# Attention in blocks of three key tiles instead of two, with VectorE adding to two heads at once

## The chip, the cores and the metric

The kernel runs on one core of one Trainium2 chip. The metric is device time in microseconds of one execution. Before the change it is 10870.94 us, the median of 3 runs (10868.82 to 10871.01).

## The reference: what is computed

Four graph layers over N = 3327 nodes of 128 features, each `x = x + layer(relu(layernorm(x)), adj)`. The change touches only the second, an attention with 128 heads of depth 8, which sees the dense adjacency matrix as a bias, added twice:

```python
q = (x @ Wq.T).reshape(d, n, h)      # d = 128 heads, n = 3327 nodes, h = 8
k = (x @ Wk.T).reshape(d, n, h)
v = (x @ Wv.T).reshape(d, n, h)
a = jnp.einsum('dnh,dmh->dnm', q, k) * scale
a = a + adj + adj
a = jax.nn.softmax(a, axis=2)
out = jnp.einsum('dnm,dmh->dnh', a, v)
```

That is 128 x 3327 x 3327 exponentials. The other layers are products with the adjacency matrix, a gated unit and a nearest-neighbour graph; they lie ahead of and behind the attention and are not touched.

## The kernel before, in words

**Tiling.** Keys lie on the 128 partitions: 26 tiles (T) of 128 keys. Queries lie along the free dimension in 7 chunks (QW = 476; the last has 471, rounded up to 472). Heads go in 32 groups of four; a head has 32 partitions of TensorE's rows (its keys in f16 high and low parts), so four heads' score products stand in separate row groups. The loops run over chunk c, group g, tile t: 7 x 32 x 26 steps (L920, L931).

**A step.** For each head of a tile, TensorE makes a 128 x 476 block of scores (L873), twice the adjacency tile `a2` (bf16, scaled) is added, ScalarE takes the exponential, and TensorE weighs the values with it into `acc` (L904; four heads in one PSUM bank, an f32 product in two passes). A column of ones among the values gives the denominators; the division comes later.

**Pairs.** Two tiles share a buffer `p8` of 8 places (4 buffers). The adjacency reaches the scores in three ways. *Early* heads, all four of the even tile and head 3 of the odd one: the product goes into one of four PSUM banks named `early`, and VectorE adds `a2` while it copies to `p8` (L876); one exponential of five heads in place (L897). *Late* heads, 0 to 2 of the odd tile: the products go into the three banks of `late` (one buffer); for `3 - n_g` of them TensorE adds the adjacency with a product by twice the identity, `two_i` (L892); one exponential straight from PSUM (L894); for the other `n_g` POOL multiplies the result by `e`, the exponential of the adjacency tile (L896). `n_g` is 2, and 1 in the first five pairs of a group of chunk 0, where POOL has other work. `e` is made by ScalarE once per odd tile and chunk, in the last group of the chunk before (`exp_of`, L557, called in L986).

```python
if t % 2 == 0:
    early = [ps.tile([P, 512], F32, name="early", bufs=4) for _ in range(4)]
...
nc.scalar.activation(p8[:, 5:8, :we], late[:, :, :we], AF.Exp, scale=1.0 / S_SCALE)
...
nc.scalar.activation(p8[:, :5, :we], p8[:, :5, :we], AF.Exp, scale=1.0 / S_SCALE)
```

**Order.** The stage is under a manual schedule (L918): each engine works its instructions in the order in which the program writes them, and semaphores hold back only what depends on another engine. A tile is weighed six tiles after its scores (`ahead`, L948). After the last tile of a group VectorE copies `acc` to `o4` (L913), which SyncE stores; the next group's first weighing waits for that copy. All eight PSUM banks are in use: 4 early, 3 late, 1 acc.

**What else is in the queues.** In chunk 0 only: each pair's keys are brought into tile order by VectorE (`key_pair`, L653; POOL does one pair in 13), seven pairs ahead, and stored for the later chunks (L620); and POOL parts the keys and queries of a coming group into f16 high and low (`Parting`, L586 and L587): loads of both raw sides behind tile 15, the parts at tiles 2 to 9, the stores behind tile 11. In all chunks but the last, POOL doubles the next chunk's adjacency tiles (L285) and sums them (L296), SyncE loads a group's queries, values and keys some tiles ahead (L951, L975).

Of the kernel before, what the change touches and what calls it, by code (L numbers as in the profile page):

```python
# [15 lines left out]
ALU = mybir.AluOpType  # L16
# [40 lines left out]
def kernel(  # L57
# [506 lines left out]
    SIDES = ((kf, kt, "k"), (qf, qt, "q"))  # L564

    class Parting:
# [8 lines left out]
        def load(self, side):  # L575
            src, _, name = SIDES[side]
            self.raw[side] = kq0.tile([E * JW, WJ], F32, name=f"raw_{name}")
            nc.sync.dma_start(self.raw[side], self.rows(src, 0))

        def part(self, side, i):  # L580
            if i == 0:
                self.hi[side] = kq0.tile([E * JW, WJ], F16, name=f"hi{side}")
                self.lo[side] = kq0.tile([E * JW, WJ], F16, name=f"lo{side}")
# [10 lines left out]
        def at(self, t):  # L594

            for side in range(2):
                t0 = 2 + 4 * side
                if t0 <= t < t0 + 4:
                    self.part(side, t - t0)
                if t == 11:  # L600
                    self.store(side)

# [43 lines left out]
    def key_pair(engine, k_ins, pairs):  # L646
# [3 lines left out]
        k = kq0.tile([P, 2, P], F16, name="k", bufs=KEYS_AHEAD + 2)  # L650
# [120 lines left out]
    early.append(lambda: (ahead_part.load(0), ahead_part.load(1)))  # L771
# [73 lines left out]
    assert T % 2 == 0  # L845
    PLACES = ((0, 1, 2, 3), (5, 6, 7, 4))
    n_groups = NH // 4
    ahead = 6
    adj_pools.append(ctx_at.enter_context(tc.tile_pool(name="at_adj1", bufs=T)))
    with tc.tile_pool(name="at_in", bufs=1) as a_pool, tc.tile_pool(name="at_p", bufs=4) as p_pool, tc.tile_pool(  # L850
# [3 lines left out]
        nc.vector.memset(acc, 0.0)  # L854

# [11 lines left out]
        def scores(step, k, q4, a2, e_a, p8, n_g):  # L867
            c, _, t = step
            we = even(c)

            def product(i, sp, stop=True):
                r = slice(32 * i, 32 * i + 32)
                nc.tensor.matmul(sp[:, :we], k[r], q4[r, :we], start=True, stop=stop)  # L873

            def add(i, sp):
                nc.vector.tensor_tensor(p8[:, PLACES[t % 2][i], :we], sp[:, :we], a2[:, :we], op=ALU.add)  # L876

            if t % 2 == 0:
                early = [ps.tile([P, 512], F32, name="early", bufs=4) for _ in range(4)]
                for i in range(4):  # L880
                    product(i, early[i])
                for i in range(4):
                    add(i, early[i])
                return
            n_i = 3 - n_g
            late = ps.tile([P, 3, 512], F32, name="late")
            early = ps.tile([P, 512], F32, name="early", bufs=4)
            for i in range(3):
                product(i, late[:, i], stop=i >= n_i)
            product(3, early)  # L890
            for i in range(n_i):
# [617 lines left out]
```

## Time and profile before

The profiled execution took 10873.82 us, its span is 10872.1 us; the runs' median is 10870.94 us. The attention stage lies between 432 and 10148 us of the span. Busy time in us by stretch (records of one engine may overlap; the union is counted):

| stretch, us | PE | DVE | ACT | POOL |
|---|---|---|---|---|
| 0 to 432, ahead of the attention | 340.95 | 248.68 | 161.92 | 114.18 |
| 432 to 1826, chunk 0 | 1324.64 | 1380.56 | 1389.39 | 1112.13 |
| 3216 to 4606, chunk 2 | 1229.39 | 1222.02 | 1390.00 | 987.11 |
| 8775 to 10148, chunk 6 (472 wide) | 1223.27 | 1209.98 | 1373.00 | 920.66 |
| 10148 to 10872, behind it | 581.53 | 418.79 | 185.07 | 119.03 |

A profile line has the line of the kernel, the engine, the operation, what it writes and reads with shapes, a count, then busy time in us, the mean length of one in ns, and the engine's idle time just ahead of it with what ended most of it. A timeline line has start and length in us; a merged line (x5) is several instructions in a row, and its length runs from the first's start to the last's end. PE is TensorE, PEld its weight loads, DVE VectorE, ACT ScalarE, SP SyncE.

### The profile page before, as it was taken

The page shows a single profiled execution, that of the slowest core. Times are in us where ns is not written, and L with a number is a line of the kernel's source. Part 1 is how long each engine was busy: PE and PEld are TensorE (multiplying, and loading weights), DVE is VectorE, ACT ScalarE, POOL GpSimd, SP SyncE. Part 2 cuts the span into 40 slices and gives each one's busy share as a digit, 9 for nine tenths or more (in the row PEclk, how much of TensorE's full clock was granted, in tenths as well). Part 3 has the DMA queues.
Part 4 walks back from the last instruction along what each step waited for, and adds up shares of the span by engine and source line. Part 5 has one row for each costly group of instructions (what it writes and reads, how often), then busy time and mean ns, then how long its engine had stood idle before and what let it go on. Part 6 is the DMA issues. An engine that isn't in the chain of part 4 may idle for free. (4 is left out here: it accounts for less than half of the span.)

```text
span 10872.1 us, 197601 instructions
## 1 busy us (share of the span) xinstructions
PE 9616.0 (88%) x76707; PEld 2303.9 (21%) x76740; DVE 9368.2 (86%) x15829; ACT 10058.4 (93%) x6276; POOL 7200.9 (66%) x4082
## 2 busy tenths in 40 slices
PE   7899999888888888888888888888888888888896
PEld 3211111111111111111111111111111111111453
DVE  5799999888888888888888888888888888888666
ACT  2799999999999999999999999999999999999432
POOL 3388887777767777677777777776777766666203
PEclk9999999999999999999999999999999999999998
DMA  8643332111111111111111111111111111111422
GB/s 295 201 107 102 100 105 80 45 44 44 41 45 44 44 42 45 43 44 42 45 46 42 41 44 45 42 45 42 44 41 45 43 38 35 38 37 35 154 98 100
DMA packets 459277, 710.11 MB, mean 65 GB/s; under 512 B 53128, under 2 KB 387967, under 8 KB 452698
## 3 DMA queue, kind: packets, MB, share of 16 engines
q1 hardware_dynamic: 455144, 690.86, 21.3%
q8 instruction: 606, 9.93, 0.4%
q0 software_dynamic: 3184, 6.51, 0.2%
q14 instruction: 343, 2.81, 0.1%
HBM read 557.43 MB, written 139.73 MB: 64 GB/s over the span
## 5 line engine op out<-in xcount | busy, mean ns | idle before, releaser
L876 DVE TENSOR_TENSOR p<-early,a 128x476 f32<-128x476 f32 (+1 forms) x14560 | 8411.0, 644 | 998.4 <-PE early L873 683.4
L897 ACT ACTIVATE p<-p 128x2380 f32<-128x2380 f32 (+1 forms) x2912 | 9230.9, 3170 | 0.0
L896 POOL TENSOR_TENSOR p<-p,e 128x952 f32<-128x952 f32 (+2 forms) x2912 | 6304.7, 2165 | 2730.9 <-ACT p L894 2617.0
L894 ACT ACTIVATE p<-late 128x1428 f32<-128x1428 f32 (+1 forms) x2912 | 6814.9, 2340 | 9.1 <-DVE p L876 7.6
L904 PE MATMUL acc<-p,v 128*9 128x476 f32 (+1 forms) x46592 | 5736.1, 564 | 80.2 <-DVE o L913 79.6
L873 PE MATMUL early<-q,k_in 32*128 32x476 f16 (+1 forms) x12480 | 2163.7, 367 | 2.1
L873 PEld LDWEIGHTS <-k_in 32*128 32x128 f16 x19968 | 707.8, 90 | 4816.7 <-issue 4816.0
L873 PE MATMUL late<-q,k_in 32*128 32x476 f16 (+1 forms) x7488 | 944.3, 365 | 882.1 <-ACT p L894 881.0
L892 PE MATMUL late<-a,two_i 128*128 128x476 bf16 (+1 forms) x3072 | 1123.7, 374 | 0.0
L904 PEld LDWEIGHTS acc<-p,v 128*9 128x9 f32 x46592 | 692.4, 88 | 1788.0 <-issue 1619.1
L873 PE MATMUL early<-q,k 32*128 32x476 f16 x2080 | 429.5, 369 | 25.6 <-DVE p L876 14.5
L892 PEld LDWEIGHTS <-two_i 128*128 128x128 bf16 x3072 | 281.3, 96 | 622.7 <-issue 622.7
L873 PEld LDWEIGHTS <-k 32*128 32x128 f16 x3328 | 111.1, 91 | 698.9 <-issue 680.3
L235 PE MATMUL agg_ps<-a,part 128*128 128x512 bf16 (+1 forms) x1067 | 226.6, 369 | 6.3 <-ACT agg L1293 3.2
L653 DVE TENSOR_REDUCE k<-k_in 128x256 f16<-128x256 f16 x377 | 221.7, 588 | 0.0
L285 POOL TENSOR_SCALAR a<-a_in 128x476 bf16<-128x476 f32 (+2 forms) x156 | 218.9, 1403 | 0.5
L348 PE MATMUL agg_ps<-a,part 128*128 128x512 bf16 (+4 forms) x720 | 172.5, 397 | 52.9 <-DMA a<-in_adjT_dram 52.0
L296 POOL TENSOR_TENSOR deg_half<-deg_half,a 128x476 f32<-128x476 f32 (+1 forms) x175 | 191.6, 1095 | 2.1
L873 PE MATMUL late<-q,k 32*128 32x476 f16 x1248 | 157.9, 368 | 37.6 <-ACT p L894 22.0
L194 ACT ACTIVATE agg<-agg_ps 128x512 f32<-128x512 f32 x9 | 4.7, 598 | 196.4 <-PE agg_ps L235 196.4
L1288 PE MATMUL sp<-yT,hT 128*128 128x512 f32 (+1 forms) x364 | 171.1, 611 | 12.1 <-ACT agg L1293 6.2
L913 DVE COPY o<-acc 105x476 f32<-105x476 f32 (+1 forms) x224 | 146.1, 652 | 21.5 <-PE acc L904 8.9
(288 smaller groups left out, 2606.5 us busy)
## 6 DMA issues: line engine op xcount, KB each, us to landing
k_in<-keyd SPq DMA_DIRECT2D x192, 832.0 KB
v<-vd SPq DMA_DIRECT2D x896, 117.0 KB
a<-in_adjT_dram SPq DMA_DIRECT2D x39, 1663.5 KB
a<-adj SPq DMA_DIRECT2D x78, 831.8 KB
a_in<-in_adjT_dram SPq DMA_DIRECT2D x125, 238.0 KB
keyd<-k SPq DMA_DIRECT2D x416, 64.0 KB
k_in<-kt SPq DMA_DIRECT2D x240, 104.0 KB
q<-qt SPq DMA_DIRECT2D x1520, 14.9 KB
```

Of the source, the lines that this page charges most:

```text
L235: nc.tensor.matmul(acc[c][:, :w], part[:, t, :], a[:, c0 : c0 + w], start=(t == 0 and i == 0), stop=(t == T - 1 and i == len(parts) - 1),)
L285: nc.gpsimd.tensor_scalar(a2[:kp, :w], a, 2.0 * S_SCALE, None, op0=ALU.mult)
L296: nc.gpsimd.tensor_tensor(deg_half[:, :w], deg_half[:, :w], a2[:, :w], op=ALU.add)
L348: nc.tensor.matmul(acc[c][:, :w], part[:kp, t, :], a16[:kp, c0 : c0 + w], start=(n == 0 and i == 0), stop=(last and i == len(parts) - 1),)
L653: nc.vector.tensor_reduce(k, src.unsqueeze(3), AX.X, ALU.max)
L873: nc.tensor.matmul(sp[:, :we], k[r], q4[r, :we], start=True, stop=stop)
L876: nc.vector.tensor_tensor(p8[:, PLACES[t % 2][i], :we], sp[:, :we], a2[:, :we], op=ALU.add)
L892: nc.tensor.matmul(late[:, i, :we], two_i, a2[:, :we], start=False, stop=True)
L894: nc.scalar.activation(p8[:, 5:8, :we], late[:, :, :we], AF.Exp, scale=1.0 / S_SCALE)
L896: nc.gpsimd.tensor_tensor(g8, g8, e_a[:, :we].unsqueeze(1).to_broadcast([P, n_g, we]), op=ALU.mult)
L897: nc.scalar.activation(p8[:, :5, :we], p8[:, :5, :we], AF.Exp, scale=1.0 / S_SCALE)
L904: nc.tensor.matmul(acc[32 * i : 32 * i + EA, :w], v4[:kp, i, t, :], p8[:kp, PLACES[t % 2][i], :w], start=(t == 0), stop=(t == T - 1),)
```

## The change

- Chunks 1 to 6 go in eight blocks of three tiles and one of two per group; chunk 0 keeps blocks of two. A block has one buffer `p_early` (up to 9 heads: all of its tiles but the last, and head 3 of the last) and one `p_late` (heads 0 to 2 of the last tile), four of each. One exponential covers all early heads of a block (9 in a triple, 5 in a pair), one its three late heads.
- In chunks 1 to 6 `n_g` is 3: POOL multiplies all late heads and no product by `two_i` is left there. `exp_of` runs for the last tile of each block only: 9 tiles a chunk.
- The four early banks become one tile `ring`, handed out bank by bank. In chunks 1 to 6 VectorE adds to two heads (two banks) in one instruction; head 3 of the last tile goes alone. In chunk 0 it adds one head at a time, as before.
- TensorE's order within a block is written out: a and A are heads 0, 1 and 2, 3 of the first tile, b and B those of the second, c is head 3 and l heads 0 to 2 of the last tile, W weighs one older tile if enough tiles lie between (7 in chunks 1 to 6, 6 in chunk 0). Triples take turns between two orders. In chunk 0 the order is aAWlcW, so that `two_i`'s product comes ahead of head 3's.
- Chunk 0's parting: parts at tiles 6 to 9 and 16 to 19, each side stored behind its parts, the second raw side loaded at tile 10 into the same buffer, the next first side at tile 20; `n_g` is 1 in the pairs of these tiles (4 in 13). The keys' pairs have 8 buffers, not 9.

The diff, cut:

```diff
         def part(self, side, i):
             if i == 0:
-                self.hi[side] = kq0.tile([E * JW, WJ], F16, name=f"hi{side}")
-                self.lo[side] = kq0.tile([E * JW, WJ], F16, name=f"lo{side}")
+                self.hi[side] = kq0.tile([E * JW, WJ], F16, name="hi")
+                self.lo[side] = kq0.tile([E * JW, WJ], F16, name="lo")
...
         def at(self, t):
 
-            for side in range(2):
-                t0 = 2 + 4 * side
+            for side, t0 in ((0, 6), (1, 16)):
                 if t0 <= t < t0 + 4:
                     self.part(side, t - t0)
-                if t == 11:
+                if t == t0 + 4:
                     self.store(side)
+            if t == 10:
+                self.load(1)
+    PARTING_TILES = (6, 7, 8, 9, 16, 17, 18, 19)
...
-        k = kq0.tile([P, 2, P], F16, name="k", bufs=KEYS_AHEAD + 2)
+        k = kq0.tile([P, 2, P], F16, name="k", bufs=KEYS_AHEAD + 1)
...
-    early.append(lambda: (ahead_part.load(0), ahead_part.load(1)))
+    early.append(lambda: ahead_part.load(0))
...
+    PAIRS = [2] * (T // 2)
+    TRIPLES = [3] * ((T - 2) // 3) + [2]
+    assert sum(PAIRS) == sum(TRIPLES) == T
+    late_tiles = [sum(TRIPLES[: i + 1]) - 1 for i in range(len(TRIPLES))]
+    PAIR_ORDER = "aAWlcW"
+    ORDERS = {(3, 0): "aWAWbWBlc", (3, 1): "cWaWAbWlB", (2, 0): "WaWAlc", (2, 1): "WcWalA"}
+    PIECES = {"a": (0, (0, 1)), "A": (0, (2, 3)), "b": (1, (0, 1)), "B": (1, (2, 3))}
...
-    ahead = 6
...
+        ring = ps.tile([P, 4, 512], F32, name="ring")
+        nc.vector.memset(ring, 0.0)
...
+        class Block:
...
+            bank = 0
...
+                self.early = p_pool.tile([P, 9, QW], F32, name="p_early")
+                self.late = p_pool.tile([P, 3, QW], F32, name="p_late")
+                self.left = 4 * (n - 1) + 1
+            def product(self, pos, i, sp, stop=True):
                 r = slice(32 * i, 32 * i + 32)
-                nc.tensor.matmul(sp[:, :we], k[r], q4[r, :we], start=True, stop=stop)
...
-            if t % 2 == 0:
-                early = [ps.tile([P, 512], F32, name="early", bufs=4) for _ in range(4)]
+                nc.tensor.matmul(sp[:, : self.we], self.keys(self.t0 + pos)[r], self.q4[r, : self.we], start=True, stop=stop)
...
+            def sums(self, pos, heads, together):
+                we, place = self.we, 4 * pos + (heads[0] if pos < self.n - 1 else 0)
+                banks = [(Block.bank + i) % 4 for i in range(len(heads))]
+                Block.bank = (Block.bank + len(heads)) % 4
+                for i, bank in zip(heads, banks):
+                    self.product(pos, i, ring[:, bank])
...
+                if together:
...
+                    n = len(heads)
+                    a2 = self.a[pos][:, :we].unsqueeze(1).to_broadcast([P, n, we])
+                    nc.vector.tensor_tensor(
+                        self.early[:, place : place + n, :we], ring[:, banks[0] : banks[0] + n, :we], a2, op=ALU.add
+                    )
+                else:
+                    for i, bank in enumerate(banks):
+                        nc.vector.tensor_tensor(self.early[:, place + i, :we], ring[:, bank, :we], self.a[pos][:, :we], op=ALU.add)
+                self.left -= len(heads)
+                if not self.left:
+                    n = 4 * (self.n - 1) + 1
+                    p = self.early[:, :n, :we]
+                    nc.scalar.activation(p, p, AF.Exp, scale=1.0 / S_SCALE)
+            def late_ones(self):
+                we, pos = self.we, self.n - 1
+                late = ps.tile([P, 3, 512], F32, name="late")
+                for i in range(3):
+                    self.product(pos, i, late[:, i], stop=i >= 3 - self.n_g)
+                for i in range(3 - self.n_g):
+                    nc.tensor.matmul(late[:, i, :we], two_i, self.a[pos][:, :we], start=False, stop=True)
+                nc.scalar.activation(self.late[:, :, :we], late[:, :, :we], AF.Exp, scale=1.0 / S_SCALE)
+                g = self.late[:, 3 - self.n_g :, :we]
+                nc.gpsimd.tensor_tensor(g, g, self.e[:, :we].unsqueeze(1).to_broadcast([P, self.n_g, we]), op=ALU.mult)
...
+            def weigh(self, pos):
+                t = self.t0 + pos
+                q0, w = q_chunks[self.c]
+                kp = rows_of(t)
...
-                    product(i, early[i])
-                for i in range(4):
-                    add(i, early[i])
-                return
-            n_i = 3 - n_g
-            late = ps.tile([P, 3, 512], F32, name="late")
-            early = ps.tile([P, 512], F32, name="early", bufs=4)
-            for i in range(3):
-                product(i, late[:, i], stop=i >= n_i)
-            product(3, early)
-            for i in range(n_i):
-                nc.tensor.matmul(late[:, i, :we], two_i, a2[:, :we], start=False, stop=True)
-            add(3, early)
-            nc.scalar.activation(p8[:, 5:8, :we], late[:, :, :we], AF.Exp, scale=1.0 / S_SCALE)
-            g8 = p8[:, 8 - n_g : 8, :we]
-            nc.gpsimd.tensor_tensor(g8, g8, e_a[:, :we].unsqueeze(1).to_broadcast([P, n_g, we]), op=ALU.mult)
-            nc.scalar.activation(p8[:, :5, :we], p8[:, :5, :we], AF.Exp, scale=1.0 / S_SCALE)
...
+                    if pos < self.n - 1:
+                        p = self.early[:, 4 * pos + i]
+                    else:
+                        p = self.late[:, i] if i < 3 else self.early[:, 4 * pos]
...
+            def events(c, g, t, n, a_in):
+                nonlocal coming, part, ahead_part, n_stored, k_next
...
+                    part.at(t)
+                    if t == 20 and g + 1 < n_groups:
+                        ahead_part = Parting((g + 3) % n_groups)
+                        ahead_part.load(0)
...
                 if t == 10 and g == 1 and c:
-                    store_sum(c, ps.tile([P, 512], F32, name="early", bufs=4), a_pool.tile([P, QW], F32, name="o4"))
+                    store_sum(c, ring[:, Block.bank], a_pool.tile([P, QW], F32, name="o4"))
...
-                if t % 2 and g == n_groups - 1 and c + 1 < len(q_chunks):
-                    e_next.append(exp_of(a_next[t], c + 1))
-            for j in range(len(steps) - ahead, len(steps)):
-                weigh(*begun.pop(j))
...
+                a_in, t0 = [], 0
+                for i, size in enumerate(TRIPLES if c else PAIRS):
+                    if c:
+                        n_g, keys, order = 3, (lambda t, k=k_now: k[:, t]), ORDERS[size, n_block % 2]
+                    else:
+                        n_g, order = 1 if t0 + 1 in PARTING_TILES else 2, PAIR_ORDER
+                        keys = lambda t, g=g: pairs[(g * T + t) // 2][:, t % 2]
+                    block = Block(c, g, t0, size, i, q4, v4, a_t, e_t[i], n_g, keys)
+                    to_weigh += [(block, pos) for pos in range(size)]
+                    ahead = 7 if c else 6
+                    heads = 0
+                    for step in order:
+                        if step == "W":
+                            if n_tiles + heads / 2 >= n_weighed + ahead:
+                                weigh_next()
+                        elif step == "l":
+                            block.late_ones()
+                        else:
+                            pos, which = PIECES[step] if step != "c" else (size - 1, (3,))
+                            heads += len(which)
+                            block.sums(pos, which, c > 0)
+                    n_tiles += size
+                    n_block += 1
+                    for t in range(t0, t0 + size):
+                        events(c, g, t, n, a_in)
+                    t0 += size
...
+                    if g == n_groups - 1 and c + 1 < len(q_chunks):
+                        while len(e_next) < len(late_tiles) and late_tiles[len(e_next)] < t0:
+                            e_next.append(exp_of(a_next[late_tiles[len(e_next)]], c + 1))
+            while to_weigh:
+                weigh_next()
```

## The prediction

> **What bounds the kernel now.** I read the page's busy shares first, then the groups by line, then the timeline of one engine at a time inside the attention stage (432 to 10148 us, 89% of the span).
>
> ```profile
> PE 9616.0 (88%) x76707; PEld 2303.9 (21%) x76740; DVE 9368.2 (86%) x15829; ACT 10058.4 (93%) x6276; POOL 7200.9 (66%) x4082
> L897 ACT ACTIVATE p<-p 128x2380 f32<-128x2380 f32 (+1 forms) x2912 | 9230.9, 3170 | 0.0
> L894 ACT ACTIVATE p<-late 128x1428 f32<-128x1428 f32 (+1 forms) x2912 | 6814.9, 2340 | 9.1 <-DVE p L876 7.6
> L876 DVE TENSOR_TENSOR p<-early,a 128x476 f32<-128x476 f32 (+1 forms) x14560 | 8411.0, 644 | 998.4 <-PE early L873 683.4
> ```
>
> Four engines are over 65% busy, but only ScalarE never waits: 0.0 and 9.1 us of idle time ahead of 5824 exponentials, against 998 us ahead of VectorE's adds. Their records overlap (3170 + 2340 ns of records in each 3.3 us), so a record's length is no price; the price is the distance from start to start. ScalarE's timeline, first near the end of chunk 0 (where L557 prepares the next chunk), then in a middle chunk, 476 queries wide, then in the last, 472 wide:
>
> ```profile
> 1787.28 1.42 ACT L557 ACTIVATE e<-a 128x476 f32<-128x476 bf16 x1
> 1787.77 2.18 ACT L894 ACTIVATE p<-late 128x1428 f32<-128x1428 f32 x1
> ...
> 3002.92 2.46 ACT L894 ACTIVATE p<-late 128x1428 f32<-128x1428 f32 x1
> 3004.16 3.29 ACT L897 ACTIVATE p<-p 128x2380 f32<-128x2380 f32 x1
> 3006.24 2.46 ACT L894 ACTIVATE p<-late 128x1428 f32<-128x1428 f32 x1
> ...
> 8999.24 2.23 ACT L894 ACTIVATE p<-late 128x1416 f32<-128x1416 f32 x1
> ...
> 9009.12 2.25 ACT L894 ACTIVATE p<-late 128x1416 f32<-128x1416 f32 x1
> ```
>
> A pair of tiles takes 1.245 us for three late heads and 2.08 for five early ones, 3.325 together (median over all pairs). The last chunk has 32 elements less per pair and its lines stand three pairs apart: 9.88 / 3 = 3.293 by these two, 3.299 over the chunk, about 0.0265 less, so an element costs 0.83 ns. I take 1/1.2 = 0.833: 1428 elements are 1.190 and leave 0.055 fixed; 2380 are 1.983 and leave 0.095; the 476 elements of L557 cost 0.49 and leave 0.093, the same as the other one that reads SBUF. So the two exponentials of a pair carry 0.15 us of fixed cost. (1.245 and 2.08 alone would also fit 0.872 ns an element and nothing fixed; the last chunk and L557 speak against that.)
>
> Now the two engines that could take over, VectorE in chunk 0 and TensorE in a middle chunk:
>
> ```profile
> 1674.47 2.90 DVE L876 TENSOR_TENSOR p<-early,a 128x476 f32<-128x476 f32 x5
> 1677.27 0.60 DVE L653 TENSOR_REDUCE k<-k_in 128x256 f16<-128x256 f16 x1
> 1677.78 2.90 DVE L876 TENSOR_TENSOR p<-early,a 128x476 f32<-128x476 f32 x5
> ...
> 4998.58 0.36 PE L873 MATMUL early<-q,k_in 32*128 32x476 f16 x1
> 4998.86 0.12 PEld L904 LDWEIGHTS acc<-p,v 128*9 128x9 f32 x8 [0.32 <-issue]
> ...
> 5003.56 0.38 PE L873 MATMUL late<-q,k_in 32*128 32x476 f16 x3
> 5003.88 0.38 PE L892 MATMUL late<-a,two_i 128*128 128x476 bf16 x1
> 5004.18 0.99 PE L904 MATMUL acc<-p,v 128*9 128x476 f32 x8
> 5005.10 0.67 PE L873 MATMUL early<-q,k_in 32*128 32x476 f16 x4
> ```
>
> Five adds start 2.80 us apart from what follows: 0.560 each, of which 476/0.96 = 0.496 are elements and 0.064 fixed. In chunk 0 a key reduction (0.505) makes VectorE's pair 3.305 of ScalarE's 3.325: there it has nothing to spare; in chunks 1 to 6 it needs 2.80. On TensorE a set of score products costs 0.3 us whether it is one head (4998.58 to 4998.86) or three or four in separate row groups, the two_i product 0.3, and weighing one tile 0.92. A pair is 0.32 + 0.30 + 0.92 + 0.30 + 0.92 = 2.76.
>
> **The change, term by term.** *ScalarE, chunks 1 to 6.* A group of 26 tiles goes from 13 pairs (13 x 3.325 = 43.225) to 8 triples and a pair. A triple has 12 x 476 = 5712 elements: 4.760 + 0.15 = 4.912 (one and a half pairs were 4.988). Group: 8 x 4.912 + 3.325 = 42.62, 0.604 less. The 472-wide chunk: 13 x 3.299 to 8 x 4.872 + 3.299, 0.612 less. 160 x 0.604 + 32 x 0.612 = **-116.2 us**. *exp_of* now runs for 9 late tiles a chunk, not 13: 6 x 4 x 0.49 = **-11.8 us**, in ScalarE's row as well.
>
> *VectorE's double add* is in no row. From below: its 952 elements alone, 0.992. From above: two singles, 1.120. The fixed part doesn't grow with size in this trace (0.064 at 476 elements; 1024 start 1.14 apart, 0.075; a 3327-element search 3.534, 0.068), and operations with an operand repeated over rows (L538, 512 elements, 687 ns) are as long as flat ones (L1157, 692). So I take 0.992 + 0.064 = 1.056. Triple: 4 x 1.056 + 0.560 = 4.784 (one and a half pairs: 4.20). Group: 34 doubles, 9 singles and the o4 copy (0.57): 35.90 + 5.04 + 0.57 = 41.5 of ScalarE's 42.62. VectorE goes from 88% to 97%: that cover is thin. With D for the double, VectorE decides once 34 D + 5.61 > 42.62, **D > 1.088**.
>
> [...]
>
> *TensorE.* The two_i product goes (n_g is 3); products come by twos and ones, so a triple needs 5 sets, 6 if none share: 5 x 0.3 + 3 x 0.92 = 4.26, to 4.56. It fits in 4.91. *POOL* multiplies three heads per triple: 1.20 for one head and 2.22 for two make 3.25 for three, of 4.91; two heads per pair were 2.22 of 3.33. The same load, hidden.
>
> *The waits.* The ring has four banks, two doubles. A product that waits for an add starts 0.05 after its end, and an add starts 0.02 after its product's. From one double's products past a W to the next is 0.3 + 0.92 = 1.22, more than a double's 1.056, so VectorE drains the ring while the Ws pass; B, l and c have no W between and refill it. The last thing TensorE waits for in a block is a W that needs the exponential of two blocks ago. Call its end 0: that W ends at 0.97, the next products are ready at 1.4, and from that add to the same place two blocks on are 8 doubles and 2 singles, 9.57 of ScalarE's 2 x 4.912 = 9.82. It closes with 0.25 us to spare, and a block's last add ends over 1 us before its exponential is due. At a group's end o4 holds the next group's first W back by 0.66, some 0.4 of it idle for VectorE in half of the groups: 41.5 + 0.2 is still under 42.62. The price of all waits I take as 0; if they cost more than the 0.9 left per group, it is theirs one for one.
>
> *Chunk 0* keeps pairs and single adds, but its two_i product now stands ahead of head 3's, which becomes a set of its own: +0.3 of TensorE per pair, 3.06, and 3.36 where n_g is 1 (4 of 13 pairs), just about what VectorE allows. Behind o4, the second W and the next products come later: 0.39 us of VectorE idle per group, 12.5 in all, against some 10 that it had left in this chunk. Bounds 0 and +13; I take **+5**. The later stores, the second raw load at tile 10 (SP then waits for POOL's parting, at most some 3 us, with a key store behind it) and the one key buffer less stay behind 7 pairs of keys made ahead: 0. The ring's memset falls into VectorE's 3.3 us wait for vd ahead of its first add: 0.
>
> Sum on the profiled execution: 10873.8 - 116.2 - 11.8 + 5 = 10751; the median of the runs lies 2.9 below it: **10748 us**, -1.1%.
>
> **The rivals.** (1) *VectorE becomes the bound, slower.* If each bank's row of a double pays its own start, D = 1.12: a group is 34 x 1.12 + 5.61 + 0.2 = 43.9, against 43.23 and the 0.2 that L557 took: +0.46 x 192 = 88, with chunk 0 some 10960. It decides from D = 1.088 and costs time over before from about 1.107. For it: no row reads two banks on VectorE. Against it: the constant 0.064. (2) *The in-order queues eat part of the gain*: TensorE stuck behind a W or l while VectorE has an empty ring. 0.3 us lost per triple beyond the spare 0.128 would cost 0.17 x 1536 = 264 and be slower; half a tenth beyond it gives 10825. For it: 97% on VectorE with two doubles of buffer; against it: 1 us of lead in each block. (3) *The ring is not a ring*: were its one tile guarded as a whole, each double would wait for the one before it, 1.056 + 0.5, a triple 7.4, the kernel some 14700. Against it: late's exponential and the adds share p8 today and overlap. (4) *No difference*: 0.872 ns an element and nothing fixed, or rival 2 at its break-even.
>
> **Numbers.** The forecast (10735 to 10765) 0.58; rival 2 with a gain left (10765 to 10849) 0.17; within 0.2% (22 us, about what a measurement of this kernel can tell from no change) 0.06; slower 0.19, nearly all of it rivals 1 and 2, 0.01 rival 3. Faster 0.75. The range runs from 10730 to 10880, into the no-change case, for 0.8.
>
> **What would show it.** Right: ScalarE's late exponentials 4.91 us apart in chunks 1 to 6 with no idle time, groups of 42.6 us, doubles starting 1.056 apart where they queue, L557 67 times in place of 91. Wrong: idle time ahead of the 4284-element exponentials ended by VectorE, doubles over 1.088 apart (rival 1), or idle VectorE ended by TensorE in every block (rival 2); chunk 0 longer than 1395 us would make that term too small.

## The result: 1.72 times as long

The changed kernel takes 18727.61 us (median of 4 runs, 18724.8 to 18757.04) against 10869.88 us before in the same series: **1.7237 times as long, 95% interval 1.7207 to 1.7266**. The prediction was 10748 us, and its range ended at 10880. The profiled execution took 18757.04 us, its span 18755.2 us.

### The profile after

First the page of the changed kernel: busy shares, the granted clock by slice (each digit a tenth of full speed), and the groups that answer to those shown of before.

```profile
PE 14168.5 (76%) x74212; PEld 2342.7 (12%) x74212; DVE 10898.8 (58%) x11606; ACT 10324.8 (55%) x4716; POOL 7264.4 (39%) x3314
...
PEclk9677776777767777767767677776777776666688
...
L904 DVE TENSOR_TENSOR p_early<-ring,a 128x952 f32<-128x952 f32 (+3 forms) x8256 | 8623.7, 1045 | 6259.2 <-PE ring L892 6169.4
...
L914 ACT ACTIVATE p_early<-p_early 128x4284 f32<-128x4284 f32 (+3 forms) x2144 | 7115.7, 3319 | 795.3 <-DVE p_early L904 794.7
L892 PE MATMUL ring<-q,k_in 32*128 32x476 f16 (+1 forms) x14784 | 3996.8, 472 | 3742.4 <-DVE p_early L904 3725.0
L923 ACT ACTIVATE p_late<-late 128x1428 f32<-128x1428 f32 (+1 forms) x2144 | 2910.0, 1357 | 6839.2 <-PE late L892 4511.9
```

No engine is busy 80% of the span any more. ScalarE, which waited 9 us before, waits 6839 us ahead of the late exponentials. VectorE and TensorE wait for each other: 6169 us of the adds' idle time ended with a product into `ring`, 3725 us of the products' idle time ended with an add. Two engines that wait by turns for each other are a ping-pong, not a pipeline. And the granted clock, 0.989 over the execution before, is 0.718.

The timeline of the changed kernel early in chunk 3 shows both. Columns: start, length, engine, line, operation, and in brackets the idle time ahead with what ended it.

```profile
8001.45 1.77 PE L936 MATMUL acc<-p_early,v 128*9 128x476 f32 x8
8001.66 1.15 DVE L904 TENSOR_TENSOR p_early<-ring,a 128x952 f32<-128x952 f32 x1 [0.77 <-PE ring L892]
8003.16 0.58 PE L892 MATMUL ring<-q,k_in 32*128 32x476 f16 x2
...
8003.78 1.15 DVE L904 TENSOR_TENSOR p_early<-ring,a 128x952 f32<-128x952 f32 x1 [0.97 <-PE ring L892]
...
8005.37 0.58 PE L892 MATMUL ring<-q,k_in 32*128 32x476 f16 x2
...
8006.06 1.15 DVE L904 TENSOR_TENSOR p_early<-ring,a 128x952 f32<-128x952 f32 x1 [1.13 <-PE ring L892]
8007.27 0.38 PE L892 MATMUL ring<-q,k_in 32*128 32x476 f16 x2 [0.35 <-DVE p_early L904]
...
8007.68 1.15 DVE L904 TENSOR_TENSOR p_early<-ring,a 128x952 f32<-128x952 f32 x1 [0.47 <-PE ring L892]
...
8008.88 0.36 PE L892 MATMUL ring<-q,k_in 32*128 32x476 f16 x1 [1.06 <-DVE p_early L904]
```

Two things are to be seen. At the end of the stretch, at full clock, the double of 8006.06 ends at 8007.21, the next products start at 8007.27, and the next double at 8007.68: one full turn of 1.62 us per double, where the prediction had 1.056 with the products hidden. Products fill two banks, yet they wait for the add that reads the *other* two. Ahead of it the same weighing of a tile takes 1.77 us, not 0.99, and two products 0.58, not 0.38: half the clock (granted 0.50 from 8001.45 to 8006.00, 1.00 from 8007 to 8009). Counted over the whole trace, **0 of 16876 products into `ring` start while an add is in flight**; before, 11420 of 14572 products into the `early` banks did. The wait stands in the trace: 9503 of the 9504 sets of products wait for the one semaphore that the adds raise, once for each set; before, each product had a wait of its own for it (14556 of 14560).

By stage (from the same trace): a group takes some 78.3 us (43.43 before), a triple 8.9 to 10.3 (mean by its place in the group), chunk 0, which has no doubles at all, 2515 us (1388 before; from the end of its first exponential of early heads to the end of its last, as everywhere below).

### The profile page after: what moved, and what is told of

Same layout as the page of the kernel before. It is cut to its first block, busy times and chain, and to the rows that moved or that the text cites. A ratio compares the mean times of both kernels' runs of the same rounds, so it can differ in the third digit from the quotient of the medians.

```text
span 18755.2 us, 183655 instructions
## 1 busy us (share of the span) xinstructions
PE 14168.5 (76%) x74212; PEld 2342.7 (12%) x74212; DVE 10898.8 (58%) x11606; ACT 10324.8 (55%) x4716; POOL 7264.4 (39%) x3314
## 5 line engine op out<-in xcount | busy, mean ns | idle before, releaser
L904 DVE TENSOR_TENSOR p_early<-ring,a 128x952 f32<-128x952 f32 (+3 forms) x8256 | 8623.7, 1045 | 6259.2 <-PE ring L892 6169.4
L925 POOL TENSOR_TENSOR p_late<-p_late,e 128x1428 f32<-128x1428 f32 (+3 forms) x2144 | 6359.3, 2966 | 10560.7 <-ACT p_late L923 10555.1
L936 PE MATMUL acc<-p_early,v 128*9 128x476 f32 (+3 forms) x33728 | 8565.8, 827 | 30.8 <-issue 30.5
L914 ACT ACTIVATE p_early<-p_early 128x4284 f32<-128x4284 f32 (+3 forms) x2144 | 7115.7, 3319 | 795.3 <-DVE p_early L904 794.7
L892 PE MATMUL ring<-q,k_in 32*128 32x476 f16 (+1 forms) x14784 | 3996.8, 472 | 3742.4 <-DVE p_early L904 3725.0
L923 ACT ACTIVATE p_late<-late 128x1428 f32<-128x1428 f32 (+1 forms) x2144 | 2910.0, 1357 | 6839.2 <-PE late L892 4511.9
L936 PE MATMUL acc<-p_late,v 128*9 128x476 f32 (+3 forms) x12864 | 3126.9, 818 | 0.0
L909 DVE TENSOR_TENSOR p_early<-ring,a 128x476 f32<-128x476 f32 x2080 | 1282.3, 650 | 1018.4 <-PE ring L892 994.3
L892 PE MATMUL ring<-q,k 32*128 32x476 f16 x2080 | 572.0, 446 | 585.0 <-DVE p_early L909 580.9
L936 PEld LDWEIGHTS acc<-p_early,v 128*9 128x9 f32 (+1 forms) x33728 | 686.3, 93 | 2248.4 <-issue 2237.6
```

What stands on the lines that cost most here:

```text
L892: nc.tensor.matmul(sp[:, : self.we], self.keys(self.t0 + pos)[r], self.q4[r, : self.we], start=True, stop=stop)
L904: nc.vector.tensor_tensor(self.early[:, place : place + n, :we], ring[:, banks[0] : banks[0] + n, :we], a2, op=ALU.add)
L909: nc.vector.tensor_tensor(self.early[:, place + i, :we], ring[:, bank, :we], self.a[pos][:, :we], op=ALU.add)
L914: nc.scalar.activation(p, p, AF.Exp, scale=1.0 / S_SCALE)
L923: nc.scalar.activation(self.late[:, :, :we], late[:, :, :we], AF.Exp, scale=1.0 / S_SCALE)
L925: nc.gpsimd.tensor_tensor(g, g, self.e[:, :we].unsqueeze(1).to_broadcast([P, self.n_g, we]), op=ALU.mult)
```

## The experiments

Three questions: is the one tile `ring` the cause, what does the clock add, and would the predicted sum hold without both? "Clock" is the mean granted clock of the profiled execution; each series ran beside the kernel before (10869.34 to 10872.58 us), and the ratios are to that.

| kernel | us | ratio, 95% interval | clock |
|---|---|---|---|
| after | 18727.61 | 1.7207 to 1.7266 | 0.718 |
| e1_two_tiles | 11358.91 | 1.0432 to 1.0467 | 0.980 |
| e2_before_ring | 14233.24 | 1.3068 to 1.3112 | 0.980 |
| e3_singles | 11870.57 | 1.0910 to 1.0946 | 0.960 |
| e4_pairs | 11669.23 | 1.0712 to 1.0747 | 0.985 |
| e5_fours | 15299.46 | 1.4031 to 1.4101 | 0.828 |
| e6_order | 11052.53 | 1.0154 to 1.0188 | 0.989 |
| e7_order_chunk0 | 11055.81 | 1.0155 to 1.0189 | 0.988 |
| e8_twice | 22064.31 | 2.0274 to 2.0342 | 0.676 |
| e9_order_ring | 20461.86 | 1.8795 to 1.8853 | 0.566 |
| e10_best | 12070.25 | 1.1086 to 1.1116 | 0.960 |
| e11_order2 | 10739.50 | 0.9862 to 0.9895 | 0.990 |
| e12_weigh_more | 16505.26 | 1.5164 to 1.5215 | 0.951 |

### The one tile

**e1_two_tiles**: the change with two tiles of two banks in turn, in place of one of four.

```diff
-                banks = [(Block.bank + i) % 4 for i in range(len(heads))]
-                Block.bank = (Block.bank + len(heads)) % 4
-                for i, bank in zip(heads, banks):
-                    self.product(pos, i, ring[:, bank])
+                two = ps.tile([P, 2, 512], F32, name="two", bufs=2)
+                for n, i in enumerate(heads):
+                    self.product(pos, i, two[:, n])
```

> The changed kernel with one edit: the four early banks are no longer one tile but two tiles of two banks, taken in turn, one for each call of sums. Theory A (the ring is guarded as one tile: a product into any of its banks waits for the last add out of any bank, TensorE and VectorE take turns, TensorE idles and its granted clock falls): products again start while an add runs, the clock is back at 0.98 to 0.99, and the time is what the blind sum gave, 10748 us (10735 to 10850). Theory B (the clock falls because products come in twos between long weighings, and the slow TensorE makes the waits): clock near 0.72 and over 16000 us still. Theory C (a double add costs as much as two singles): clock up, but VectorE bound, about 10960 us.

11358.91 us, above theory A's range: 7369 us of the 7858 lost come back by this edit alone, and the clock with them. (A single now takes a slot of two banks, not one; e9 below changes the tile with the slots kept.) 12431 of 16876 products now start with an add in flight, queued doubles start 1.047 to 1.057 us apart. The waits view of e1:

```profile
PE two L888 <- DVE p_early L898: 987.5, 1518, 1.0
DVE p_early L898 <- PE two L888: 548.0, 1021, 1.5
```

The ping-pong is down from 6169 and 3725 us to 548 and 988; 4.5% is still lost against before, and has another cause.

**e2_before_ring**: the other way round, the kernel *before* with its four early banks made one tile, and nothing else.

```diff
+        ring = ps.tile([P, 4, 512], F32, name="ring")
...
-                early = [ps.tile([P, 512], F32, name="early", bufs=4) for _ in range(4)]
+                early = [next_bank() for _ in range(4)]
```

> The kernel before with one edit: its four early banks become one tile of four banks, handed out bank by bank in the same order; pairs, single adds and all else stay. Theory A: the guard alone makes the slowness. With a full clock a pair would take two waits for products (0.44 each), four adds in a row (2.32) and the fifth (0.64), 3.84 us in place of 3.325, or 12370 us; with the clock falling as in the changed kernel 13000 to 16500. No product into the ring starts while an add runs (in the kernel before 11408 of 14556 did). Theory B: no difference, 10870 us, clock 0.99.

14233.24 us, with 0 of 14572 products during an add and a pair of 4.43 us, where 3.84 had been worked out: the direction is right, the price is larger. The waits view of e2:

```profile
DVE p L882 <- PE ring L879: 3867.6, 5566, 2.5
PE ring L879 <- DVE p L882: 3711.6, 2898, 7.4
```

The clock stays at 0.98, so this is the price of the guard by itself: 31% on a kernel in which not one instruction has changed its work or place. Both signs of the edit agree: banks that are slices of one tile are guarded together.

**e5_fours**: the change, with the products of a tile issued four at a time: three turns per triple in place of five.

```diff
-    ORDERS = {(3, 0): "aWAWbWBlc", (3, 1): "cWaWAbWlB", (2, 0): "WaWAlc", (2, 1): "WcWalA"}
+    ORDERS = {(3, 0): "fWWgWlc", (3, 1): "cWfWWlg", (2, 0): "WfWlc", (2, 1): "WcWlf"}
+    PIECES = {"f": (0, (0, 1, 2, 3)), "g": (1, (0, 1, 2, 3))}
```

> The changed kernel, ring still one tile of four banks, but the products of a tile go in fours ahead of its adds (two doubles in chunks 1 to 6, four singles in chunk 0), so a triple has three turns between TensorE and VectorE in place of five, a pair of chunk 0 two in place of three. If the price of the guard is one wait of about 0.5 us a turn, and TensorE's clock falls only where a 3.4 us window is busy for less than about 0.6 (e2_before_ring: 0.63 and a clock of 0.98), a triple takes 3 x 0.5 + 4.784 = 6.3 us at a clock of 0.95 or more: 12900 to 13800 us. If the clock falls because of anything else in the new blocks (the order of the weighings, three heads late at once, no two_i product), it stays at 0.72 and the time over 16000.

15299.46 us. It is faster than the change, as the guard has it, but the clock of 0.828 was not foreseen, and the time is past the top of the range by 1500 us. As turns and clock both differ from the change's, this run does not give the price of a turn.

### What is left without the guard

**e3_singles** (e1 with single adds) and **e4_pairs** (e1 with pairs in all chunks) were to part the doubles from the triples.

```diff
-                            block.sums(pos, which, c > 0)
+                            block.sums(pos, which, False)
```
```diff
-                for i, size in enumerate(TRIPLES if c else PAIRS):
+                for i, size in enumerate(PAIRS):
```

> As e1_two_tiles, but VectorE adds one head at a time in chunks 1 to 6 too (nine adds of 0.560 in a triple). If a double costs 1.056, this one has 8 x 5.04 + 2.80 + 0.57 = 43.7 us of VectorE in a group against 42.62 of ScalarE, so VectorE bounds it and it is about 0.9 x 192 = 180 to 200 us slower than e1_two_tiles: about 10940 us. If a double costs as much as two singles (theory C), it takes the same time as e1_two_tiles, both near 10950.

> As e1_two_tiles, but blocks of two tiles in all chunks (13 per group; doubles, the late heads all on POOL, exp_of for 13 tiles). It leaves out the triples alone. If ScalarE's fixed cost per exponential is 0.15 us per pair and ScalarE stays the bound, a pair takes 3.325 us again: 10870 to 10885 us, about 128 us more than e1_two_tiles. If ScalarE has no fixed cost (0.872 ns an element), it takes the same time as e1_two_tiles but for the 12 us of exp_of.

Both missed: singles cost 512 us over e1, pairs 310. They don't part what they were to part, since either edit also changes when buffers come free. In e4 a new wait leads the view:

```profile
DVE p_early L898 <- PE acc L930: 2072.1, 2474, 3.1
```

That is VectorE waiting for a weighing to give back a `p_early` buffer. What they do show is that going back to single adds or to pairs does not bring e1's remaining loss back. That the loss lies in the order of the queues is shown by e6 and e11 below.

**e6_order**: e1 with one order for every triple and the weighings two further behind. In chunk 0, e6 keeps two slots; **e7_order_chunk0** gives chunk 0 back four one-bank tiles and puts head 3's product ahead of `two_i`'s, as before.

```diff
-    ORDERS = {(3, 0): "aWAWbWBlc", (3, 1): "cWaWAbWlB", (2, 0): "WaWAlc", (2, 1): "WcWalA"}
+    ORDERS = {(3, 0): "aWAbWBlcW", (3, 1): "aWAbWBlcW", (2, 0): "aWAlcW", (2, 1): "aWAlcW"}
...
-                    ahead = 7 if c else 6
+                    ahead = 9 if c else 6
```
```diff
-    PAIR_ORDER = "aAWlcW"
+    PAIR_ORDER = "fWmW"
```

> e1_two_tiles with another order in chunks 1 to 6: a W A b W B l c W in every triple, a W A l c W in the last block of two, weighing nine tiles behind. In e1_two_tiles VectorE waits 548 us for products, because a double needs 1.056 us of VectorE while a product and a weighing need 1.22 of TensorE, three times in a row, and because two head-3 products meet. With no two weighings in neighbouring steps a triple is worked out at 4.9 to 5.0 us, a group at 43 to 44 with the o4 copy: 10800 to 11000 us. If the stalls come from something else (two slots are too few whatever the order), it stays at 11300 to 11400.

> e6_order with chunk 0 as the kernel before has it: four early tiles of one bank each, head 3's product ahead of two_i's, adds one by one. e1_two_tiles lost 29 us in chunk 0 (1416 us against 1388 in the kernel before). If two slots and the place of two_i's product cost that, this one is 25 to 35 us faster than e6_order; if the moved parting or the one key buffer less cost it, no faster.

e6: 11052.53 us, just above its range. By place in the group the blocks take 4.913, 4.912, 5.630, 4.955, 5.10 (four times) and 3.322 us (medians); a group takes 44.22 on average. The first two are the predicted 4.912, the last the predicted 3.325; the third is the one in which the copy `o4` stands ahead of a weighing. The timeline of e6 shows what the ring was to be: products of 8005.78 and 8007.00 start inside a row of adds that has no gap.

```profile
8005.64 5.59 DVE L898 TENSOR_TENSOR p_early<-two,a 128x476 f32<-128x476 f32 x6
8005.78 0.38 PE L888 MATMUL two<-q,k_in 32*128 32x476 f16 x2
8006.08 0.98 PE L930 MATMUL acc<-p_early,v 128*9 128x476 f32 x8
...
8007.00 0.84 PE L888 MATMUL two<-q,k_in 32*128 32x476 f16 x4
```

e7: 11055.81 us, chunk 0 1420 us as in e6 (1416.5), 1388 before. So chunk 0's 30 us are neither the two slots nor the place of `two_i`.

**e10_best** and **e11_order2** go after the copy. Chunk 0 weighs one tile further behind in both; chunks 1 to 6 differ.

First e10 against e7, then e11 against e10:

```diff
-    ORDERS = {(3, 0): "aWAbWBlcW", (3, 1): "aWAbWBlcW", (2, 0): "aWAlcW", (2, 1): "aWAlcW"}
+    ORDERS = {(3, 0): "aAWbWBlWc", (3, 1): "aAWbWBlWc", (2, 0): "aAWlWc", (2, 1): "aAWlWc"}
...
-                    ahead = 9 if c else 6
+                    ahead = 10 if c else 7
```
```diff
-    ORDERS = {(3, 0): "aAWbWBlWc", (3, 1): "aAWbWBlWc", (2, 0): "aAWlWc", (2, 1): "aAWlWc"}
+    ORDERS = {(3, 0): "aAWbWBWlc", (3, 1): "aAWbWBWlc", (2, 0): "aWAlcW", (2, 1): "aWAlcW"}
...
-                    ahead = 10 if c else 7
+                    ahead = 7
```

> e7_order_chunk0 with the order of a block changed and the queue of weighings one longer (10 in chunks 1 to 6, 7 in chunk 0), so that the last tile's weighing falls on a pair's second place and the copy of the output (o4) is over before the next group's first weighing. Theory that the 0.7 us per group (0.9 in chunk 0) left in e6_order is the wait for that copy: a triple 4.79 to 4.91, a group 42.7 to 43.2, chunk 0 back to about 1390, 10,745 to 10,850 us in all. Rival, that the two tiles in turn are the rest: 10,900 to 11,050 us.

> e10_best with the order of a triple changed to aAWbWBWlc, of the last pair back to aWAlcW, and the queue of weighings 7 everywhere. A model of the three in-order queues with the measured durations (set of products 0.30, weighing 0.92, double 1.056, single 0.56, copy of the output 0.57, exponentials at 1/1.2 ns per element, 0.055 from end to start) gives e6_order's triples as measured (4.91, 4.91, 5.55, 4.94, 5.10 x 4 against 4.913, 4.912, 5.630, 4.955, 5.10 x 4) and for this order 4.91 at every place, a group 42.6 and the weighings' wait for the copy hidden. With chunk 0 at 1386 as in e10_best: 10,740 to 10,790 us. Rival, that some wait that the model lacks (loads, partings, key sums on these engines) takes over: 10,800 to 11,000 us.

e10 hits for chunk 0 (1386 us) and misses for the rest: groups of 49.7 to 50.2 us, the loss in the first three blocks (6.63, 6.39, 6.92). Its waits view has

```profile
DVE p_early L900 <- PE acc L950: 856.5, 565, 2.5
```

All of this wait falls in the first three blocks, some 1.5 us of a group in each. With ten tiles behind, the four buffers are all held when a new group begins. The wait that an order takes away at the copy, a longer queue brings back at the buffers.

e11: **10739.50 us, ratio 0.9878 (0.9862 to 0.9895), faster than both kernels.** The triples take 4.913 to 4.915 us (median by place), a group 42.80 on average. In chunks 1 to 6, e11 differs from e1 in the two order strings alone, its queue of 7 included: there the order by itself takes a group from 45.9 to 42.8 us, some 580 us of the kernel. The page of e11:

```profile
PE 9573.0 (89%) x74179; PEld 2170.7 (20%) x74212; DVE 10153.6 (95%) x11605; ACT 9933.4 (93%) x4716; POOL 7302.1 (68%) x3314
...
L900 DVE TENSOR_TENSOR p_early<-two,a 128x952 f32<-128x952 f32 (+3 forms) x8256 | 8012.4, 1037 | 91.7 <-PE two L890 59.9
L920 ACT ACTIVATE p_early<-p_early 128x4284 f32<-128x4284 f32 (+3 forms) x2144 | 7755.7, 3617 | 0.0
...
L935 ACT ACTIVATE p_late<-late 128x1428 f32<-128x1428 f32 (+1 forms) x2144 | 3535.0, 1649 | 13.2 <-DVE p_early L910 7.5
```

ScalarE is without waits again (0.0 and 13.2 us), and VectorE at 95% waits 92 us in all for its doubles. ScalarE's timeline of e11 has the late exponentials 4.91 us apart:

```profile
8004.20 1.57 ACT L935 ACTIVATE p_late<-late 128x1428 f32<-128x1428 f32 x1
8005.44 3.99 ACT L920 ACTIVATE p_early<-p_early 128x4284 f32<-128x4284 f32 x1
8009.11 1.57 ACT L935 ACTIVATE p_late<-late 128x1428 f32<-128x1428 f32 x1
```

### The clock

**e8_twice**: the change, with each set of products into `ring` issued twice.

```diff
-                for i, bank in zip(heads, banks):
-                    self.product(pos, i, ring[:, bank])
+                for _ in range(2):
+                    for i, bank in zip(heads, banks):
+                        self.product(pos, i, ring[:, bank])
```

> The changed kernel with every score product into the ring issued twice (the second writes the same scores again): work added, nothing taken away; it is there to keep TensorE busy in the turns. If the low clock is TensorE's idle time, a turn at full clock becomes 0.3 longer (1.6 to 1.9) with TensorE busy for 1.5 of it, over 0.6, the clock comes back over 0.9, and the kernel gets faster than the changed one though it does more: 17000 to 18300 us. If the clock doesn't depend on how busy TensorE is, each of about 9700 turns costs 0.3 to 0.6 more: 21000 us or more.

22064.31 us at a clock of 0.676: this many more products do not hold the clock, they only lengthen the turns.

**e9_order_ring**: e6 on halves of one four-bank tile.

```diff
-                two = ps.tile([P, 2, 512], F32, name="two", bufs=2)
+                two = ring[:, 2 * (Block.turn % 2) : 2 * (Block.turn % 2) + 2]
+                Block.turn += 1
```

> This is e6_order with its two two-bank tiles replaced by halves of one four-bank tile (chunk 0 alike); every instruction and its place in the order are e6_order's, weighings spread evenly between the products. If the four-bank tile makes each set of products wait for the last add of the other half (guard theory), turns of 1.6 us (double) and 1.25 us (copy) follow each other: a triple 1.6 x 4 + 1.25 = 7.65 us, a group about 66 us, chunk 0 1900 to 2500 us, and no product starts during an add. What the clock does tells two causes apart: if it falls only in stretches without weighings, it stays at or above 0.95 here and the time is 15,300 to 16,400 us; if TensorE's average share of busy time decides (4.3 / 7.65 = 0.56), the clock is near 0.7 and the time over 18,000 us. If the one tile is not the cause, 11,050 us as e6_order.

20461.86 us, 1.85 times e6, with every instruction in e6's place: again the tile alone, and 0 of 16876 products start during an add. Of the two readings of the clock in the expectation, the one by stretches without weighings fails: the weighings are spread evenly here, and the clock, 0.566, falls lower than in the change. The one by TensorE's average busy share has the direction and a time over 18,000 us, but put the clock near 0.7. From chunk 1 on most triples take 10.27 us, and nearly all of it is at half speed:

```profile
PEclk8777765555555555555555555555555555555578
```

**e12_weigh_more**: e9, with up to two weighings of a triple issued a second time (R) where TensorE would wait for an add.

```diff
-    ORDERS = {(3, 0): "aWAbWBlcW", (3, 1): "aWAbWBlcW", (2, 0): "aWAlcW", (2, 1): "aWAlcW"}
+    ORDERS = {(3, 0): "aWARbWBRlcW", (3, 1): "aWARbWBRlcW", (2, 0): "aWARlcW", (2, 1): "aWARlcW"}
...
+                        elif step == "R":
+                            if weighed[0] in blocks[-4:]:
+                                weighed[0].weigh(weighed[1], True)
```

> e9_order_ring, one tile of four banks as there, with up to two weighings per triple issued a second time in the places where TensorE otherwise waits for an add (after A and after B), so that those tiles count twice in the sums: its output differs from the reference in that. Some 1.8 us more of TensorE per triple, none of it on the chain of turns at full clock (0.30 + 0.92 is less than a turn's 1.6). If the clock is what a TensorE that is too often idle loses, and the weighings are what holds it, the clock in chunks 1 to 6 comes back to at least 0.95 and a group takes the guard's own 66 to 68 us in place of 88: 16,200 to 17,000 us, some 20% faster than e9_order_ring with more work. If the clock falls for another reason (the ring's banks, or the load itself), it stays near 0.57 and the time rises above 21,000 us.

16505.26 us: **24535 more matmuls than e9, and 3957 us (19%) less time.** The page of e12, and two lines of its waits view:

```profile
PE 13741.8 (83%) x98747; PEld 2960.8 (18%) x98780; DVE 10879.4 (66%) x11605; ACT 10172.3 (62%) x4716; POOL 7286.5 (44%) x3314
...
PEclk9777777999999999999999999999999999999998
...
DVE p_early L901 <- PE ring L890: 4098.6, 8063, 2.0
...
PE ring L890 <- DVE p_early L901: 1879.3, 4911, 1.3
```

The clock is low in chunk 0, where nothing was added, and full from chunk 1 on. Groups take 66.8 us, and the waits for `ring` remain; the timeline of e12 gives the pure turn of the guard, 1.62 us from double to double:

```profile
8007.37 0.38 PE L890 MATMUL ring<-q,k_in 32*128 32x476 f16 x2 [0.40 <-DVE p_early L901]
...
8007.78 1.15 DVE L901 TENSOR_TENSOR p_early<-ring,a 128x952 f32<-128x952 f32 x1 [0.47 <-PE ring L890]
8008.98 0.38 PE L890 MATMUL ring<-q,k_in 32*128 32x476 f16 x2 [0.32 <-DVE p_early L901]
...
8009.40 1.15 DVE L901 TENSOR_TENSOR p_early<-ring,a 128x952 f32<-128x952 f32 x1 [0.47 <-PE ring L890]
```

This parts the loss in two, as an estimate: if the change's groups took e12's 66.8 us at full clock, and its chunk 0 the 1890 us of e2 (clock 0.98), the guard would be 192 x (66.8 - 43.4) + (1890 - 1388), about 5000 of the 7858 us, and the clock the other 2900. The orders of e12 and e2 are not quite the change's; how far off the split is, no run shows.

## Why the prediction was wrong

**The step that failed is "The price of all waits I take as 0"**, in the paragraph on the waits. It follows products and adds through "The ring has four banks, two doubles", and so takes each bank to be guarded by itself. It is not: the products of one double wait for the add of the other (0 of 16876 start during an add; e1, e2 and e9 change the tiles and move the time by 7369, 3362 and 9409 us). With that the 1.056 us of a double become a turn of 1.62, the 0.560 of a single a turn that makes a pair 4.43 us in e2, and VectorE's 0.128 us of spare time per triple is lost in the first turn. The same step fails a second time, for the order: where it has B, l and c refill the ring and closes with 0.25 us to spare, e1, with the change's order and no guard across its tiles, takes 45.9 us a group and not 42.62.

**Rival 3 named the mechanism and was given 0.01.** The evidence that put it there, "late's exponential and the adds share p8 today and overlap", is true of the trace, but it is of writers and readers of separate parts of a buffer in SBUF, and says nothing of products and adds on a PSUM tile. The trace of before could not settle it: the one PSUM tile of several banks in its attention, `late`, is read by one exponential as a whole. It was an unknown of the kind that is to be bounded from both sides, and only one bound went into the range. Its price was short as well: 7.4 us a triple and 14700 in all leave out chunk 0 (its single adds go through the ring too, +1127 us) and the clock.

**The clock was taken as given.** It stood at full speed in all but the first windows of the attention before, and nothing in the prediction asked what holds it there. That is the second factor: 78 us a group where the turns alone make some 67.

**What held**, seen once the guard and the order are out of the way:
- The exponentials: 4.912 us per triple predicted, 4.913 to 4.915 measured in e11, with 0.15 of fixed cost for two; the pair 3.325 and 3.326. A group 42.62 plus `exp_of`'s share of 0.14 against 42.80.
- The double: D = 1.056 taken, 1.046 to 1.057 from start to start in a queue in e1, e6 and e11 (records of 1.15 overlap). Its 0.96 elements a ns is, as an estimate, the slope from 0.560 us at 476 elements to 3.534 at 3327, both from start to start in the trace of before. Rival 1 with D = 1.12 is out.
- TensorE's 4.26 to 4.56 us per triple fits in 4.91 in e11 (busy 89%), and POOL's load stays hidden (68%).
- The sum: 10748 predicted, 10739.50 for e11, which does what the arithmetic assumed. In parts it is less close, and some of the agreement is luck: chunks 1 to 6 gain 119 us where 128 were forecast, chunk 0 gains 2 where 5 were to be lost, and some 17 us, in no term, come from outside the chunks.

**What was mis-sized beside it.** Chunk 0's "+5 (bounds 0 to +13)" measures +28 in e6 and +32 in e7: behind the copy the weighing of a group's last tile falls on the first place of a pair, and the next group waits for it, some 0.9 us a group and not 0.39. One more tile of distance takes it away (1386 us in e10 and e11, 2 less than before). And the order of the change is not free even with separate tiles: e1's 45.9 us a group against e11's 42.8, rival 2's mechanism, 488 us over before where it had set some 264 as its slower case. Some 30 of the 488 us are chunk 0's. The rest lies in chunks 1 to 6, where the order is the one thing in which e11 differs from e1.

**Left open.** A four-bank tile with each bank guarded by itself was not tried, nor a double that spans two separate one-bank tiles. The 17 us or so by which e11's profiled execution gains more than its seven chunks show (138 against 121) lie outside the chunks: some 12 ahead of the first exponential of early heads (at 436.4 us before, 424.8 in e11), the rest behind the last. They were not followed.

## What to carry to other kernels

Before counting on a ring, ask at which grain it is guarded: look in the trace for a producer that starts while a consumer of another part of the same tile is in flight, and where the trace has no such tile, keep the case of turn by turn in the range with its full price. Slots that must overlap want tiles of their own; here that one declaration is worth 7369 us. Where the arithmetic leaves an engine only a few per cent, the order of the in-order queues and the distance of the dependent work decide whether the sum comes true (11359, 11053, 12070 and 10740 us for nearly the same instructions in other orders), and a waiting TensorE can lose its clock besides (0.718 in the change, 0.566 in e9).

## What the runs showed of the hardware that was not expected

**The granted clock halves under a busy TensorE.** In the traces it takes only the values 1.0 and 0.5 in the attention and changes in steps of 3.413 us. Counted over such windows in a stretch inside the attention of each kernel; "weighing" is the share of a window that records of weighings cover, "falls" are full windows with a half one behind them:

| kernel | windows at full, of all | falls | full windows: TensorE busy, weighing | half windows: busy, weighing |
|---|---|---|---|---|
| before | 2197 of 2197 | 0 | 0.885, 0.590 | none |
| e11_order2 | 2194 of 2197 | 3 | 0.898, 0.600 | 0.971, 0.752 |
| e2_before_ring | 3029 of 3106 | 55 | 0.700, 0.441 | 0.976, 0.689 |
| e12_weigh_more | 3315 of 3369 | 46 | 0.849, 0.622 | 0.991, 0.783 |
| after | 1711 of 4248 | 1093 | 0.563, 0.288 | 0.875, 0.637 |
| e8_twice | 1736 of 4981 | 997 | 0.634, 0.281 | 0.876, 0.499 |
| e9_order_ring | 137 of 4688 | 72 | 0.604, 0.368 | 0.800, 0.523 |

In after, e1, e2, e5 and e8 together a window at full speed with under 0.29 of weighings (all 128 rows) is the one after which the clock falls, and one at half speed with over 0.69 the one after which it returns (97 and 94% of the windows fall on the right side). By TensorE's whole busy share the best thresholds sort 90% of each. Both were found by searching thresholds, so these are correlations. The two runs that add work do not part them: e8's products leave the full windows busy for 0.634 and they fall, e12's weighings raise both shares, to 0.849 and 0.622, and the clock stays. e9's half windows, at 0.523, hardly ever come back (4551 of 4688 windows are half ones): once it has slipped, this kernel stays slow, busy 80% of its time. That the share of weighings is larger ahead of a return than ahead of a fall is in part the longer records: a weighing takes 1.77 us at half and 0.99 at full clock, so that 0.69 at half is the work of some 0.39 at full, an estimate. Whether the clock follows rows, elements or all busy time, these runs do not settle.

In the change the longest pause between two matmuls in the counted stretch (3000 to 17500 us of the span) is 1.54 us, and the clock falls 1093 times: 4586 shorter pauses (median 0.85 us, one in ten over 1.25) go with it.

**The guard goes with the tile, not with the bank.** It is a wait for a semaphore, carried by 9503 of 9504 sets of products in the trace of after; what the chip does without it no run shows. In none of the six runs with `ring` that were counted (after, e2, e5, e8, e9, e12) does a product start while an add is in flight; with separate tiles it happens thousands of times (12431 in e1).
